# A preln graph network on one core: the mask by TensorE, more PSUM banks, ranks and single graphs at the end, and a later due time for the squares

## The chip, the cores and the metric

The kernel runs on one core of a Trainium2 chip. The metric is the device time of one execution in microseconds. A core has five engines with a queue each: TensorE (PE; its weight loads are listed as PEld), VectorE (DVE), ScalarE (ACT), GpSimd (POOL) and SyncE (SP), which here issues all DMA transfers.

## The reference

There are 128 independent graphs of 128 nodes with 256 features. Layer 0 is a gated graph network of three steps, layer 1 is graph attention, and each has a layer norm with a relu in front and a residual around it.

```python
h = relu(layernorm(x))
for i in range(3):                                   # layer 0
    m = h @ weight[i]
    aggr = einsum('bst,bsd->btd', adj != 0, m)
    h = gru_cell(aggr, h, w_ih, w_hh, b_ih, b_hh)
x = x + h
h = relu(layernorm(x))                               # layer 1
Wh = h @ W.T
e = leaky_relu((Wh @ a1)[:, :, None] + (Wh @ a2)[:, None, :], 0.2)
att = softmax(where(adj == 0, -inf, e), axis=-1)
out = x + where(adj == 0, 0, att) @ Wh
```

All data are float32; the adjacency is an int32 array of zeros and ones.

## The kernel before

**Groups.** Four graphs make a group (G = 4), so there are 32 groups (NG = 32). A group passes three recurrent steps and then an epilogue, which is layer 1. Up to six groups are alive at a time, and a fixed plan interleaves their steps. The state of a group is kept in columns: `hT` has features on the partitions and nodes along the free axis.

**The recurrent step** (`gru_step`). The products with the gate weights are done by Strassen's scheme on halves, so there are 192 blocks of seven products. Each product is a run of matmuls `128x256` (L690) into one of five fixed PSUM banks: `u`, `m7` (shown as m), `c2`, `c1_0`, `c1_1` (shown as c). ScalarE copies between banks and applies tanh (the copies at L710, L713, L721; the gates r at L743 and z at L778; the candidate at L642). VectorE adds banks (L716, L725), adds the state's half to the candidate (L785) and makes the new state `hT` in three passes (L647, L649, L651). The other three PSUM banks are a rotating room named `misc` for all other TensorE results.

**The epilogue** (`epilogue`). For the last three groups (`late`, g >= 29) all turning between layouts goes through TensorE; for the others it goes by VectorE's 32x32 transposes and a way through DRAM. The steps, with names as the profile shows them:

- `pr_o` (L489): the state turned into rows, and `xt += pr_o` (L901), the residual.
- `st_b`, `mv_b`, `norm_b` (L415, L417, L421 on VectorE, L423 to L427 on GpSimd): the statistics. `h_b` (L440): the normalised rows, on ScalarE.
- `s` (L922): the two scores of each node, products with `wa`, summed by VectorE.
- `ps` (L931): the scores of the neighbours, spread over all partitions by four TensorE transposes. For the groups before 29 this goes by way of a DRAM line.
- `e` (L958): Prelu of the sum of both scores. `A` (L967) is then turned from 0/1 into -1e30/0, and added to `e` (L969). `soft` (L975): the row maximum. `e` (L979): the exponential with its sum.
- `pp` (L988) and `prT` (L992): the attention square turned by TensorE and copied (late groups). For the others `squares_by_blocks` turns it by VectorE into `prT` and a way through DRAM: `z_e<-prT`, then `e<-z_e`.
- `pq` (L598, `gathered`): the aggregation. `hs` (L1019): its copy by ScalarE. `po` (L1027): the product with `gwt`, two graphs to a bank. `xt` or `x` (L1036): scaled and added to the residual. The rows go `out` by SyncE.

The epilogue of the last group (31) runs as two tasks of two graphs each.

**What sets the order.** An account written in the kernel (`class Order`) fixes the order of all instructions while the program is built. Every step of every task states an engine, a length, the time when its inputs are ready, and the room that it needs. The account holds a time at which each engine comes free. Tasks have ranks; at equal start the smaller rank goes first. The recurrent products are laid down one after another, and between two of them `order.fill` puts whatever can start on the other engines, and `order.matmuls` puts TensorE steps whose inputs are ready by the account:

```python
def matmuls(self, most):
    end = self.free[PE] + most
    ...
            if engine != PE or self.free[PE] >= end:
                continue
            if self.begin(PE, *needs) <= self.free[PE] + 0.05:
                self.issue(task)
```

So the account's times decide only the order. Once on the chip, each engine goes through its queue in this order and waits on semaphores. After the plan has ended, `order.finish()` lays down the rest.

For the squares the account counts four transfers of `SMALL = 0.67` us issue time, `LAND = 2.5` us, four of 0.42 and again 2.5.

Of the kernel before, what the change touches and what calls it, by code (L numbers as in the profile page):

```python
# [11 lines left out]
ALU = mybir.AluOpType  # L12
# [15 lines left out]
def preln_gnn_kernel(  # L28
# [140 lines left out]
    INF = float("inf")  # L169

    class Order:
        def __init__(self):
# [28 lines left out]
        def open(self, room, name):  # L201
            self.room_of[name] = room, self.next[room]
            self.next[room] = (self.next[room] + 1) % len(self.rooms[room])
            if room == "misc":
                return ps_misc.tile([P, T], F32, tag="misc", name=name)
            if room == "h":
                return work.tile([P, G, D], F32, tag="h", name=name, bufs=ROWS)
            if room in ("prT", "e"):
                return work.tile([P, G, P], F32, tag=room, name=name)
            if room == "x1":  # L210
                return io.tile([P, G, D], F32, tag="x1", name=name, bufs=2)
            return work.tile([P, C, T], F32, tag=room, name=name)
# [266 lines left out]

    def to_rows(hT, ready, name, pairs=range(G // 2)):  # L480

        banks = []
        t = yield PE, 0.44 * len(pairs), ready, "misc", len(pairs)
        for half in pairs:
            pt = order.open("misc", f"pr_{name}_{half}").rearrange("p (k d) -> p k d", d=D)
            for k in range(2):
                for c in range(C):
                    n = half * 2 + k
                    put(nc.tensor.transpose(  # L489
                        pt[:, k, c * P : (c + 1) * P], hT[:, c, n * P : (n + 1) * P], ident  # L490
                    ))
            banks.append(pt)
        return banks, t
# [85 lines left out]
    def rows(s, ready, name):  # L579
# [3 lines left out]
        for half, pt in enumerate(banks):  # L583
            t = yield (ACT, 0.57, ready) if half else (ACT, 0.57, ready, "h")
            order.close(f"pr_{name}_{half}", t)
            if h is None:
# [51 lines left out]
    def state(s, o, old, new, v, z, ready):  # L638
# [5 lines left out]
        if len(s.halves) == C:  # L644
# [10 lines left out]
            if s.l < NL:  # L655
# [149 lines left out]
    class Group:  # L805


        def __init__(self, g):
            self.g, self.l, self.entered, self.aT = g, 0, False, None
            (self.xt, _), (self.at, self.at_ready) = xts.pop(g), ats.pop(g)  # L810
            self.scales = scales.pop(g)
            self.kept, self.prT = [], None
            self.e = self.hs = None
            self.due = False
# [29 lines left out]
    def prologue(s):  # L844
# [27 lines left out]

    def epilogue(s, pairs, ready):

        g = s.g
        graphs = range(2 * pairs[0], 2 * pairs[-1] + 2)
# [3 lines left out]
        name = f"{g}_{pairs[0]}"  # L880
# [4 lines left out]
        end = g >= NG - 2  # L885
        e_room, hs_room = (None, None) if end else ("e", "hs")
        if late:
            banks, ready = yield from to_rows(s.hT, ready, f"{name}_o", pairs)
        else:
# [5 lines left out]
        x1 = s.x1  # L895
        for half in pairs:
            t = yield (DVE if late else DVE2), 0.62, ready
            k2 = slice(half * 2, half * 2 + 2)
            if late:
                order.close(f"pr_{name}_o_{half}", t)  # L900
                put(nc.vector.tensor_add(x1[:, k2, :], x1[:, k2, :], banks[half - pairs[0]]))  # L901
            else:
# [7 lines left out]
        one, two = v[:, 0, :], v[:, 1, :] if late else score_tiles[g % 2][:, 0:G]  # L910
        ready = t
        for i in (1, 0):
            for k in graphs:
# [6 lines left out]

                unused = s.prT[:, part.start : part.start + 2, :].rearrange("p k s -> p (k s)")
                put(nc.vector.scalar_tensor_tensor(  # L922
# [4 lines left out]
        if late:  # L927
            t = yield PE, graph_t, t, "misc"
            p2 = order.open("misc", f"ps2_{name}")
            for k in graphs:  # L930
# [73 lines left out]
        banks, ready = yield from gathered(h, prT, t, f"pq_{name}", graphs)  # L1004
        final = pairs[-1] + 1 == G // 2
        if final:
# [3 lines left out]
        for c, pq in enumerate(banks):  # L1010
            t = yield (ACT, bank_t, ready, hs_room) if s.hs is None else (ACT, bank_t, ready)
            order.close(f"pq_{name}_{c}", t)
# [8 lines left out]
        for half in pairs:  # L1021
            t = yield PE, 1.73, ready, "misc"
            po = order.open("misc", f"po_{g}_{half}").rearrange("p (k d) -> p k d", d=D)
            for j in range(2):
                k = half * 2 + j
                for c in range(C):
# [3 lines left out]
                    ))  # L1030
            if final and half == pairs[-1] and not end:
                order.close(f"hs_{g}", t)
            for j in range(2):
                k = half * 2 + j
                t2 = yield DVE, 0.4, t
                put(nc.vector.scalar_tensor_tensor(  # L1036
                    x1[:, k, :], po[:, j, :], rs[:, k : k + 1], x1[:, k, :], ALU.mult, ALU.add
                ))
            order.close(f"po_{g}_{half}", t2)
        t = yield SP, 0.45, t2  # L1040
# [93 lines left out]
    for slot, (g, l) in enumerate(plan):  # L1134
# [9 lines left out]
        last = s.state = gru_step(s, last)  # L1144
        settle(True)
    order.finish()

# [35 lines left out]
```

## Time and profile before

| | us |
|---|---|
| median of three runs | 2139.47 |
| lowest and highest run | 2136.89 and 2141.38 |
| the profiled execution | 2138.47 |
| its span in the profile | 2136.7 |
| TensorE busy in the span | 2119.0 |
| VectorE, ScalarE busy | 1724.6, 1302.4 |
| DMA, share of 16 engines' span (the queue of SyncE) | 43.9% |

The busy time of TensorE is modelled from the start of each matmul, since matmuls overlap in the array; a wait shorter than the overlap does not show as idle time. The profile has 40 slices, and the granted TensorE clock is given in each; it is at nine tenths or more in all of them, with a mean of 0.999. The kernel's lines in the views are those of the file before the change; the change shifts the later ones.

### The profile page before, as it was taken

To read this page: it belongs to the slowest core of one execution; us is meant where nothing else is said; L and a number is where in the kernel's file an instruction comes from. 1 tells how busy PE (TensorE), PEld (TensorE's weight loads), DVE (VectorE), ACT (ScalarE), POOL (GpSimd) and SP (SyncE) were. 2 spreads that over 40 slices of the span, in tenths; PEclk is the share of its full clock that TensorE was granted. 3 is DMA by queue.
4 is the path that set the end of the run, shared out by engine and by line. 5 is a ranking of instruction groups with operands and counts; after the bars stand their busy time and mean duration, and the time that the engine had idled before them with its cause. 6 is when DMAs were issued, how large, how long until landed. Compare 5 with 4: busy or idle time off the path is not lost.

```text
span 2136.7 us, 32121 instructions
## 1 busy us (share of the span) xinstructions
PE 2119.0 (99%) x10763; PEld 1879.0 (88%) x10763; DVE 1724.6 (81%) x3763; ACT 1302.4 (61%) x2855; POOL 105.9 (5%) x204
## 2 busy tenths in 40 slices
PE   9999999999999999999999999999999999999997
PEld 7888888888888888888888888888888888888886
DVE  7777888788888888888888788888878887887777
ACT  6556566566666666665666566556656665665665
POOL 2000000000000000000000000000000000000000
PEclk9999999999999999999999999999999999999999
DMA  5333454444554273544445453734445354443301
GB/s 158 64 85 81 88 118 93 110 102 92 128 110 113 59 166 68 118 94 114 101 88 129 100 123 67 156 73 115 94 109 109 85 129 102 100 94 80 83 26 40
DMA packets 667942, 211.93 MB, mean 99 GB/s; under 512 B 578304, under 2 KB 644608, under 8 KB 667776
## 3 DMA queue, kind: packets, MB, share of 16 engines
q1 hardware_dynamic: 667776, 209.87, 43.9%
q8 instruction: 85, 1.39, 0.3%
q14 instruction: 81, 0.66, 0.1%
HBM read 121.91 MB, written 87.88 MB: 98 GB/s over the span
## 4 chain that ended last, share of the span: by engine, by line
PE 96%; DMA 1%; ACT 1%; DVE 1%; SPq 1%; issue 0%; POOL 0%; DVEq 0%; ACTq 0%; POOLq 0%
PE c L690 34%; PE u L690 34%; PE m L690 11%; PE pa L598 8%; PE po L1027 5%; PE pq L598 3%; PE pw L357 1%; SPq L60 1%; DMA e<-z_e 1%; DMA z_e<-prT 0%; ACT e L979 0%; DMA wih<-in_w_ih_t 0%; ACT v L642 0%; PE pr_o L489 0%; DVE v L785 0%
## 5 line engine op out<-in xcount | busy, mean ns | idle before, releaser
L778 ACT ACTIVATE z<-c,brz 128x256 f32<-128x256 f32 x384 | 185.3, 482 | 300.1 <-PE c L690 155.4
L690 PE MATMUL u<-t_h,s_hh 128*128 128x256 f32 x1152 | 343.3, 380 | 0.5 <-DVE c L716 0.3
L690 PE MATMUL u<-t_a,s_f 128*128 128x256 f32 x1152 | 311.3, 379 | 0.0
L690 PE MATMUL c<-aT,s_f 128*128 128x256 f32 x1152 | 311.3, 379 | 0.0
L743 ACT ACTIVATE r<-c,brz 128x256 f32<-128x256 f32 x384 | 175.6, 478 | 208.4 <-PE c L690 132.0
L716 DVE TENSOR_TENSOR c<-u,m 128x512 f32<-128x512 f32 x192 | 134.0, 698 | 144.9 <-PE u L690 144.7
L690 PEld LDWEIGHTS c<-aT,s_f 128*128 128x128 f32 x1152 | 218.9, 190 | 29.8
L690 PEld LDWEIGHTS u<-t_a,s_f 128*128 128x128 f32 x1152 | 218.9, 190 | 29.8
L690 PEld LDWEIGHTS u<-t_h,s_hh 128*128 128x128 f32 x1152 | 217.3, 190 | 31.5 <-DVE c L716 1.6
L785 DVE TENSOR_TENSOR v<-v,c 128x256 f32<-128x256 f32 x384 | 154.2, 420 | 110.6 <-ACT z L778 57.7
L690 PE MATMUL c<-hT,s_hh 128*128 128x256 f32 x768 | 228.4, 379 | 0.0
L721 ACT COPY c<-u 128x512 f32<-128x512 f32 x192 | 109.4, 570 | 117.3 <-PE u L690 116.9
L713 ACT COPY m<-m 128x512 f32<-128x512 f32 x192 | 112.5, 586 | 112.0 <-PE m L690 112.0
L750 ACT ACTIVATE v<-c,bhn 128x256 f32<-128x256 f32 x384 | 172.3, 477 | 0.0
L690 PE MATMUL m<-t_h,s_hh 128*128 128x256 f32 x576 | 171.5, 379 | 0.0
L690 PE MATMUL c<-t_h,s_hh 128*128 128x256 f32 x576 | 171.3, 379 | 0.0
L690 PEld LDWEIGHTS c<-hT,s_hh 128*128 128x128 f32 x768 | 145.8, 190 | 19.8
L725 DVE TENSOR_TENSOR c<-u,m 128x512 f32<-128x512 f32 x192 | 132.0, 687 | 37.5 <-ACT c L721 36.0
L690 PE MATMUL m<-t_a,s_f 128*128 128x256 f32 x576 | 155.6, 379 | 0.0
L690 PE MATMUL u<-aT,s_f 128*128 128x256 f32 x576 | 155.6, 379 | 0.0
L690 PE MATMUL c<-t_a,s_f 128*128 128x256 f32 x576 | 155.6, 379 | 0.0
L710 ACT COPY c<-u 128x512 f32<-128x512 f32 x192 | 109.5, 570 | 53.3 <-PE u L690 53.3
(125 smaller groups left out, 3900.0 us busy)
## 6 DMA issues: line engine op xcount, KB each, us to landing
z<-tq SPq DMA_DIRECT2D x248, 128.0 KB
h<-z SPq DMA_DIRECT2D x248, 128.0 KB
xt<-in_x SPq DMA_DIRECT2D x31, 512.0 KB
z_a<-tq_a SPq DMA_DIRECT2D x120, 128.0 KB
hT_a<-z_a SPq DMA_DIRECT2D x120, 128.0 KB
z_b<-tq_b SPq DMA_DIRECT2D x116, 128.0 KB
h_b<-z_b SPq DMA_DIRECT2D x116, 128.0 KB
x<-in_x SPq DMA_DIRECT2D x29, 512.0 KB
```

The lines of the kernel that those rows point to most:

```text
L598: put(nc.tensor.matmul(pa[:, k * P : (k + 1) * P], h[:, k, c * P : (c + 1) * P], A[:, k, :], start=True, stop=True,))
L690: put(nc.tensor.matmul(to(q), S[0][:, gate_no, weight, :], moving, start=first and q == 0 and i == 0, stop=(i == len(ends) - 1), skip_grou ...
L710: put(nc.scalar.copy(c1[0], u))
L713: put(nc.scalar.copy(m, m7))
L716: put(nc.vector.tensor_tensor(c2, u, m, ALU.add))
L721: put(nc.scalar.copy(c1[1], u))
L725: put(nc.vector.tensor_tensor(c22, u, m, ALU.add))
L743: put(nc.scalar.activation(r[:, o, cols], src, AF.Tanh, bias=brz[:, o : o + 1], scale=0.5))
L750: put(nc.scalar.activation(v[:, o, cols], src, AF.Identity, bias=bhn[:, o : o + 1], scale=0.5))
L778: put(nc.scalar.activation(z[:, o, cols], src, AF.Tanh, bias=brz[:, C + o : C + o + 1], scale=0.5))
L785: put(nc.vector.tensor_tensor(v[:, o, cols], v[:, o, cols], src, ALU.add))
L1027: put(nc.tensor.matmul(po[:, j, :], hs[:, c, k * P : (k + 1) * P], gwt[:, c, :], start=(c == 0), stop=(c == C - 1),))
```

## The change

The diff has six parts.

1. **The mask by TensorE** (groups 30 and 31, `end`). The mask is turned into -1e30/0 by a task of its own (`mask`, rank 1) that the account places from 5 us before the state is done. A matmul of the identity with the mask opens the bank of the scores, and the neighbours' scores are then ordinary matmuls that accumulate onto it. The add of the mask to `e` on VectorE is gone for these two groups. The transposes of the scores become ordinary matmuls in group 29 too.
2. **More banks at the end.** Once the last recurrent step is laid down, its five banks join the room `misc`, which then has eight.
3. **Ranks.** The epilogues of groups 30 and 31 have rank 1.8 and that of group 29 has 1.9, in place of 2.
4. **Single graphs in group 31**: `po`, its output add and its store go graph by graph, and the second `hs` of each half is copied by VectorE. The halves of the group stay: graphs 0 and 1, and graphs 2 and 3; pairs are now named by lists of graphs.
5. **Squares.** In `squares_by_blocks` the account's time for the landing of the turned square is 2.0 us later. This concerns groups 0 to 28.
6. `to_rows` counts its length by graphs, which gives the same numbers for pairs.

```diff
+    more = u, m7, c2, *c1
...
+            if room == "misc" and self.room_of[name][1] > 2:
+
+                return more[self.room_of[name][1] - 3].rearrange("p n t -> p (n t)")
...
 (squares_by_blocks)
-        return (yield from by_way_of_dram(
+        t = yield from by_way_of_dram(
             tmp.rearrange("p q k a -> p (q k) a"), lambda: e.rearrange("p k s -> p (k s)"),
             G, t, f"{name}_e",
-        ))
+        )
+        return t + 2.0
...
-                pairs = range(G // 2)
-                for p in [pairs] if s.g < NG - 1 else [pairs[:1], pairs[1:]]:
-                    order.add(2, epilogue(s, p, max(s.halves)))
+                if s.g >= NG - 2:
+                    s.off_ready = INF
+                    order.add(1, mask(s, max(s.halves) - 5.0))
+
+                for graphs in [range(G)] if s.g < NG - 1 else [range(2), range(2, 4)]:
+                    order.add((1.8 if s.g >= NG - 2 else 1.9 if s.g == NG - 3 else 2), epilogue(s, graphs, max(s.halves)))
...
+    def mask(s, ready):
+
+        t = s.off_ready = yield DVE, 0.36, ready
+        put(nc.vector.tensor_scalar(s.A, s.A, -1.0, BIG, ALU.add, ALU.mult))
+        return t
...
-            t = yield PE, graph_t, t, "misc"
+            t = yield PE, 4 * graph_t if end else graph_t, max(t, s.off_ready), "misc"
             p2 = order.open("misc", f"ps2_{name}")
+            if end:
+
+                put(nc.tensor.matmul(
+                    p2[:, cols], ident, s.A[:, part, :].rearrange("p k s -> p (k s)"),
+                    start=True, stop=False, skip_group_check=True,
+                ))
             for k in graphs:
-                put(nc.tensor.transpose(
-                    p2[:, k * P : (k + 1) * P], two[:, k : k + 1].to_broadcast([P, P]), ident
+                put(nc.tensor.matmul(
+                    p2[:, k * P : (k + 1) * P], two[:, k : k + 1].to_broadcast([P, P]), ident,
+                    start=not end, stop=True, skip_group_check=True,
                 ))
...
-        off_ready = yield DVE, 0.36 * n / G, ready
-        off = s.A[:, part, :]
-        put(nc.vector.tensor_scalar(off, off, -1.0, BIG, ALU.add, ALU.mult))
-        t = yield DVE2, row_t, max(t, off_ready) - HOP
-        put(nc.vector.tensor_tensor(le, le, off, ALU.add))
+        if not end:
+            off_ready = yield from mask(s, ready)
+            t = yield DVE2, row_t, max(t, off_ready) - HOP
+            put(nc.vector.tensor_tensor(le, le, s.A, ALU.add))
...
+            on = DVE if c and final_one else ACT
+            t = yield (on, bank_t, ready, hs_room) if s.hs is None else (on, bank_t, ready)
...
-            put(nc.scalar.copy(hs[:, c, cols], pq[:, cols]))
+            copy = nc.vector.tensor_copy if on == DVE else nc.scalar.copy
+            put(copy(hs[:, c, cols], pq[:, cols]))
...
-        for half in pairs:
-            t = yield PE, 1.73, ready, "misc"
-            po = order.open("misc", f"po_{g}_{half}").rearrange("p (k d) -> p k d", d=D)
+        for ks in twos(graphs) if not final_one else [range(k, k + 1) for k in graphs]:
+            t = yield PE, 0.865 * len(ks), ready, "misc"
+            po = order.open("misc", f"po_{g}_{ks[0]}").rearrange("p (k d) -> p k d", d=D)
...
+            if final_one:
+                yield SP, 0.45, t2
+                dma(out[g * G + k], x1[:, k, :])
+        if final_one:
+            return
...
+    order.rooms["misc"] += [max(order.free[PE], t) for t in (banks["u"], *3 * [0.0], banks["c1_1"])]
     order.finish()
```

More of the change, by code (lines that the diff above doesn't have):

```diff
@@ L478, in to_columns, with twos, to_rows @@
         return hT, t
-    def to_rows(hT, ready, name, pairs=range(G // 2)):
+    def twos(graphs):
+        return [graphs[i : i + 2] for i in range(0, len(graphs), 2)]
+    def to_rows(hT, ready, name, graphs=range(G)):
         banks = []
-        t = yield PE, 0.44 * len(pairs), ready, "misc", len(pairs)
-        for half in pairs:
-            pt = order.open("misc", f"pr_{name}_{half}").rearrange("p (k d) -> p k d", d=D)
-            for k in range(2):
+        t = yield PE, 0.22 * len(graphs), ready, "misc", len(twos(graphs))
+        for two in twos(graphs):
+            pt = order.open("misc", f"pr_{name}_{two[0]}").rearrange("p (k d) -> p k d", d=D)
+            for k, n in enumerate(two):
                 for c in range(C):
-                    n = half * 2 + k
                     put(nc.tensor.transpose(
@@ L584, in rows @@
             t = yield (ACT, 0.57, ready) if half else (ACT, 0.57, ready, "h")
-            order.close(f"pr_{name}_{half}", t)
+            order.close(f"pr_{name}_{2 * half}", t)
             if h is None:
@@ L811, in __init__ @@
             self.scales = scales.pop(g)
+            self.off_ready = 0.0
             self.kept, self.prT = [], None
@@ L871, in place_of_e, with epilogue @@
         ).rearrange("p (k s) -> p k s", s=P)
-    def epilogue(s, pairs, ready):
+    def epilogue(s, graphs, ready):
         g = s.g
-        graphs = range(2 * pairs[0], 2 * pairs[-1] + 2)
         n = len(graphs)
@@ L879, in epilogue @@
         cols = slice(part.start * P, part.stop * P)
-        name = f"{g}_{pairs[0]}"
+        name = f"{g}_{graphs[0]}"
         bank_t, row_t, graph_t = 0.57 * n / G + 0.02, 0.62 * n / G + 0.02, 0.11 * n
         late, h = g >= NG - 3, None
-        end = g >= NG - 2
+        end, final_one = g >= NG - 2, g == NG - 1
         e_room, hs_room = (None, None) if end else ("e", "hs")
         if late:
-            banks, ready = yield from to_rows(s.hT, ready, f"{name}_o", pairs)
+            banks, ready = yield from to_rows(s.hT, ready, f"{name}_o", graphs)
         else:
@@ L895, in epilogue @@
         x1 = s.x1
-        for half in pairs:
-            t = yield (DVE if late else DVE2), 0.62, ready
-            k2 = slice(half * 2, half * 2 + 2)
+        for i, two in enumerate(twos(graphs)):
+            t = yield (DVE if late else DVE2), 0.31 * len(two), ready
+            k2 = slice(two[0], two[-1] + 1)
             if late:
-                order.close(f"pr_{name}_o_{half}", t)
-                put(nc.vector.tensor_add(x1[:, k2, :], x1[:, k2, :], banks[half - pairs[0]]))
+                order.close(f"pr_{name}_o_{two[0]}", t)
+                put(nc.vector.tensor_add(
+                    x1[:, k2, :], x1[:, k2, :], banks[i][:, 0 : len(two), :]
+                ))
             else:
@@ L911, in epilogue @@
         ready = t
+        place = min(part.start, G - 2)
         for i in (1, 0):
@@ L919, in epilogue @@
                     s.prT = order.open("prT", f"prT_{g}")
-                unused = s.prT[:, part.start : part.start + 2, :].rearrange("p k s -> p (k s)")
+                unused = s.prT[:, place : place + 2, :].rearrange("p k s -> p (k s)")
                 put(nc.vector.scalar_tensor_tensor(
@@ L927, in epilogue @@
         if late:
-            t = yield PE, graph_t, t, "misc"
+            t = yield PE, 4 * graph_t if end else graph_t, max(t, s.off_ready), "misc"
             p2 = order.open("misc", f"ps2_{name}")
+            if end:
+                put(nc.tensor.matmul(
+                    p2[:, cols], ident, s.A[:, part, :].rearrange("p k s -> p (k s)"),
+                    start=True, stop=False, skip_group_check=True,
+                ))
             for k in graphs:
-                put(nc.tensor.transpose(
-                    p2[:, k * P : (k + 1) * P], two[:, k : k + 1].to_broadcast([P, P]), ident
+                put(nc.tensor.matmul(
+                    p2[:, k * P : (k + 1) * P], two[:, k : k + 1].to_broadcast([P, P]), ident,
+                    start=not end, stop=True, skip_group_check=True,
                 ))
@@ L1004, in epilogue @@
         banks, ready = yield from gathered(h, prT, t, f"pq_{name}", graphs)
-        final = pairs[-1] + 1 == G // 2
+        final = graphs[-1] + 1 == G
         if final:
@@ L1010, in epilogue @@
         for c, pq in enumerate(banks):
-            t = yield (ACT, bank_t, ready, hs_room) if s.hs is None else (ACT, bank_t, ready)
+            on = DVE if c and final_one else ACT
+            t = yield (on, bank_t, ready, hs_room) if s.hs is None else (on, bank_t, ready)
             order.close(f"pq_{name}_{c}", t)
@@ L1018, in epilogue @@
             hs = s.hs
-            put(nc.scalar.copy(hs[:, c, cols], pq[:, cols]))
+            copy = nc.vector.tensor_copy if on == DVE else nc.scalar.copy
+            put(copy(hs[:, c, cols], pq[:, cols]))
         ready = t
-        for half in pairs:
-            t = yield PE, 1.73, ready, "misc"
-            po = order.open("misc", f"po_{g}_{half}").rearrange("p (k d) -> p k d", d=D)
-            for j in range(2):
-                k = half * 2 + j
+        for ks in twos(graphs) if not final_one else [range(k, k + 1) for k in graphs]:
+            t = yield PE, 0.865 * len(ks), ready, "misc"
+            po = order.open("misc", f"po_{g}_{ks[0]}").rearrange("p (k d) -> p k d", d=D)
+            for j, k in enumerate(ks):
                 for c in range(C):
@@ L1030, in epilogue @@
                     ))
-            if final and half == pairs[-1] and not end:
+            if final and ks[-1] == graphs[-1] and not end:
                 order.close(f"hs_{g}", t)
-            for j in range(2):
-                k = half * 2 + j
+            for j, k in enumerate(ks):
                 t2 = yield DVE, 0.4, t
@@ L1038, in epilogue @@
                 ))
-            order.close(f"po_{g}_{half}", t2)
+            order.close(f"po_{g}_{ks[0]}", t2)
+            if final_one:
[3 more added lines that the diff above has]
+            return
         t = yield SP, 0.45, t2
```

## The prediction

> **What bounds the kernel now.** The times are those of one profiled execution: 2138.47 us on the device, 2136.7 us of it span, so 1.8 us lie around the span. The median of the runs shown, 2139.47, is 1.0 us above it. All sums below start from 2138.47; "faster" and "slower" are against 2139.47, and 0.2% of that, 4.3 us, is about what a measurement of this kernel can tell from no change.
>
> The first view to read is the head of the page.
>
> ```profile
> span 2136.7 us, 32121 instructions
> PE 2119.0 (99%) x10763; PEld 1879.0 (88%) x10763; DVE 1724.6 (81%) x3763; ACT 1302.4 (61%) x2855; POOL 105.9 (5%) x204
> ```
>
> TensorE is busy for all but 17.7 us. So an edit can gain only where TensorE waits, and every instruction added to it costs its own length unless it falls into such a wait. The second view is the busy time by stretches of the span; its columns are PE, PEld, DVE, ACT, POOL, the granted clock (PEclk), DMA.
>
> ```profile
> 0.00:20.00 20.00, 17.24 (x65) 11.70 (x66) 11.41 (x43) 9.56 (x23) 3.19 (x12) 1.00 0.89 276
> ...
> 100.00:2000.00 1900.00, 1896.82 (x9670) 1691.80 (x9669) 1547.34 (x3311) 1167.34 (x2545) 84.54 (x162) 1.00 0.46 102
> ...
> 2101.00:2137.00 36.00, 24.56 (x126) 18.93 (x124) 23.78 (x77) 16.88 (x52) 2.66 (x6) 0.95 0.13 45
> ```
>
> The waits are 2.8 us at the start (not touched), 3.2 us in the 1900 us of the middle, and 11.4 us after the last recurrent product. The third view says who ends them: columns are total us, number, longest.
>
> ```profile
> ...
> PEld pq L598 <- DMA e<-z_e: 5.1, 5, 2.2
> ...
> PE pp L988 <- ACT e L979: 4.3, 3, 2.7
> PE pq L598 <- DMA e<-z_e: 3.0, 4, 1.8
> PE pq L598 <- ACT prT L992: 2.3, 4, 0.7
> ```
>
> In the middle it is one thing: the matmul pq waits for the turned square e to come back from DRAM. The other two rows belong to the end. The chain that ended last shows the end in order (start, length, what):
>
> ```profile
> 2083.08 1.78 PE pq L598 x16
> ...
> 2098.70 2.60 PE c L690 x12
> ...
> 2106.13 3.60 PE pq L598 x16
> 2109.73 0.45 PE pr_o L489 x4
> ...
> 2120.58 3.29 PE po L1027 x14
> ...
> 2132.60 0.48 DVE xt L1036
> ```
>
> The last recurrent product ends at 2101.30. The last row is the first of two output adds; the second ends at 2133.47 in the timeline, 32.2 us after 2101.30. These 32.2 us are the tail. The same sixteen pq instructions take 1.78 us at 2083 and 3.60 at 2106. Short stretches say why:
>
> ```profile
> 2102.60:2106.00 3.40, 1.31 (x4) 0.55 (x4) 3.26 (x6) 2.98 (x11) 0.00 (x0) 1.00 0.00 0
> 2106.00:2109.40 3.40, 3.27 (x15) 3.27 (x16) 3.17 (x12) 0.67 (x2) 0.00 (x0) 0.50 0.00 0
> ...
> 2112.80:2116.20 3.40, 2.21 (x11) 1.47 (x9) 3.37 (x8) 2.03 (x7) 1.25 (x3) 1.00 0.00 0
> ```
>
> After 3.4 us with TensorE busy for 1.31, the clock is granted at 0.50 for the next 3.4. After 3.4 us with 2.21 busy it is not. The half-speed stretch cost 3.60 - 1.78 = 1.8 us, and it delayed the transposes pr_o that everything of group 31 waits for.
>
> **1. Squares 2.0 us later in the account.** The account (not the chip) decides behind which recurrent product pq is queued. One product is six records in 1.29 us. Two more microseconds put pq one or two products later, 1.3 to 2.6 us. The price of the waits: the PE row shows 3.0 us in four. A 128x256 record is 0.38 long while records start 0.216 apart (1.29 / 6), so each gap is shown 0.16 too short: 3.0 + 4 x 0.16 = 3.6, and the fifth wait, which only the PEld row counts, is about 0.3 more. That makes 4.0 us; the ends are 3.0 (PE row) and 5.1 (PEld row). The longest wait, 1.8 + 0.16, could leave 0.7 behind if pq moves by one product only. I take -4.0. The edit renumbers the whole schedule from group 2 on, transfers included: in SyncE's queue the loads of x and of the adjacency change places with the line of scores. The recurrent TensorE work of the middle is the same, instruction for instruction. New waits are taken at nothing, because in the profile no other load is waited for by TensorE in the middle; their bound is one wait such as the longest, +2.
>
> **2. What TensorE gets more of.** A transpose of 128x128 is one record of 0.11 us (pr_o, four in 0.45). An ordinary f32 matmul is two (pq, eight matmuls, sixteen records in 1.78). The score transposes of groups 29, 30 and 31 become ordinary matmuls: 4 x 0.11 = 0.44 more each. The mask matmul of 512 columns is not in the trace; twice a 256-column matmul (2 x 2 x 0.216) is 0.87, for groups 30 and 31. Together 3 x 0.44 + 2 x 0.87 = 3.1 us. In the changed program's order, pp and pq of group 29 (0.44 + 1.78) stand in front of the last recurrent product, where they stood behind it, and so do group 29's scores. That product therefore ends 2.22 + 0.44 = 2.66 us later. The rest of the additions fall into the tail.
>
> **3. The tail by steps**, from the end of the last recurrent product, durations from the rows of the same instructions before. One half of the last tanh (0.6) now runs ahead of the last z, so the three passes that make hT end at 5.45 instead of 6.02. The transposes pr_o find TensorE idle (it has done po of group 29 at 1.73, into a bank of its own): 0.60 + 0.04, to 6.1; before, they waited for pq until 8.43. Add and statistics of two graphs on VectorE take 2.18 (2110.20 to 2112.38), to 8.3; those of the other two, now queued directly behind, to 10.4. Group 30's maximum 0.68, four exponentials 1.7, last transpose and copy 1.0: 13.8. Here the mask's add (0.68) is gone and its tensor_scalar (0.42) is done earlier, in VectorE's wait for the transposes. Then TensorE works without pause: pq30 1.78, half of po29 1.73, half of po30 1.73, pp31 0.22, mask and scores of the last pair 0.87: 20.1. Two Prelu 0.63, maximum 0.42, two exponentials 0.89 and hand-offs 0.2: 22.3; TensorE meanwhile has 2.6 us of po30 and pq31, to 22.7. Then pp 0.22, one graph of po 0.87, pq 0.89, three graphs of po 2.6, drain 0.15: 27.4. The last add begins there and ends 0.5 later: 27.9, against 32.2 before. The same adding-up comes out 0.6 short for the tail of before, so I make it 28.5. The two halves of hs on VectorE instead of ScalarE, and four stores of one graph instead of two of two, are taken at nothing; the last store is smaller, the issues 0.4 each are hidden between adds 0.87 apart; bounds -0.5 and +0.5.
>
> TensorE's clock comes on top. The new order leaves TensorE idle for 3.7 us before pr_o and for about 3 before pp of group 30, longer than the 2.7 that halved the clock before. One half-speed stretch does 1.7 us of work in 3.4: +1.7 at most, of which 0.7 hides behind VectorE if it falls on group 30's scores. None costs 0, two cost 3.4; I take 1.4. Tail: 28.5 + 1.4 = 29.9, 2.3 less than 32.2.
>
> A page speaks against this order: the Trainium skill, "TensorE: Matmul & The Clock Gate", Part 1 (the HAM clock gate) says that a window of about 3.4 us without matmuls halves the clock and that a busy window restores it, the windows running freely. The trace agrees on the length, 3.4 us at 0.50; it is stricter in that 1.31 us of modelled work in the window did not prevent it. By the page alone only a wholly empty window would count, and the sum would be 1.4 lower.
>
> **Sum.** 2138.47 - 4.0 + 2.66 - 2.3 = 2134.8. The end itself is about even (2.66 - 2.3 = +0.4); the gain is the squares.
>
> **The rivals.** *The clock decides the end.* Idle stretches of 3.7 and 3 us each close the gate, the second on the unbroken run pq30 to scores of group 31: 2 us more than taken, 2136.8. For it: both gaps exceed the earlier one. Against it: the phase of the stretches is a matter of chance, and the stretch with 2.21 us of work stayed at full clock. *The waits stay.* If pq moves by one product only and the transfers it waits for move along with it, only the end counts: 2138.9. Against it: the waits before are mostly far below one product. *The end runs at full clock*, and the runs away from the profiled one lose more than 4.0 to the squares (their median is 1.0 higher): 2133. *Slower: another load becomes the late one.* The state in columns, hT_a, comes back through DRAM in the same SyncE queue. In the new order its first reader on VectorE (L458 before) stands closer behind its load in every third group. VectorE is strictly in order and 81% busy, so the wait holds back the sums c (L716) that TensorE's next product needs. Seven groups of about 1.5 us would be 10 us: 2145. It decides as soon as that load lands after its reader's turn by more than about a microsecond; for it speaks only that SyncE's queue changes everywhere, against it that no such wait stands in the profile and TensorE itself needs that state tens of microseconds later.
>
> **How the numbers follow.** Forecast (squares' waits gone, end about even) 0.62: of it 0.48 lie below 2135.2 and 0.14 above. Full clock at the end 0.07, faster. Clock decides 0.17 and waits stay 0.05, both within 0.2%. Another load late 0.09, slower. So faster 0.55, within 0.36, slower 0.09. The range: -4.0 may be -5.1 and the clock 0 instead of 1.4, with 0.8 for the stores and the run's own spread: 2131.5. Upwards the clock's 2 us, the wait that stays 0.7 and a new wait of 2: 2139.5. The slow rival and thin ends, under 2 in 10, stay outside.
>
> **What would show it.** Right: no row of pq waiting for e<-z_e, PE idle below 1 us between 100 and 2000; the last recurrent product ends 1 to 2 us earlier than 2101.3 (2.66 later by work, 4.0 earlier by waits); last add 29 to 31 us after it; PEclk 0.50 in a stretch of the last 30 us. Wrong: DVE or PE waiting for hT_a or h loads in the middle, pq still waiting, or a second half-speed stretch under pq of group 30.

## The result and the profile after

| | before | after |
|---|---|---|
| median (22 runs each, taken in turn), us | 2138.63 | 2142.02 |
| lowest and highest run | 2136.89 and 2142.62 | 2139.37 and 2146.18 |
| span of the profiled execution | 2136.7 | 2139.7 |
| last recurrent product ends | 2101.30 | 2106.64 |
| from there to the end of the last add (the tail) | 32.2 | 30.3 |

The changed kernel takes 1.0014 times as long (95% interval 1.0008 to 1.002): 3.4 us slower. The forecast was 2134.8, with a range up to 2139.5. The last two rows say where it went: the tail is shorter, as forecast (29.9), but it begins 5.3 us later, where the forecast had it begin 1.3 us earlier.

The head of the page after:

```profile
span 2139.7 us, 32130 instructions
PE 2119.6 (99%) x10781; PEld 1881.5 (88%) x10781; DVE 1724.7 (81%) x3761; ACT 1301.5 (61%) x2853; POOL 104.2 (5%) x204
```

TensorE has 18 records more and 3.0 us more span, yet only 0.6 us more busy time. The busy time by stretches (PE first; the clock, the DMA share and GB/s at the end of a row):

```profile
100.00:2000.00 1900.00, 1893.50 (x9648) 1687.66 (x9648) 1545.21 (x3307) 1165.67 (x2545) 84.31 (x162) 1.00 0.46 102
2101.00:2140.00 39.00, 28.42 (x150) 24.22 (x148) 25.33 (x77) 16.76 (x47) 2.27 (x6) 0.91 0.16 54
```

The middle was to lose less than 1 us; it loses 6.5, against 3.2 before. (The middle is the stretch from 100 to 2000 us.) Who ends the waits (total us, number, longest; lines after the change are 5 to 27 higher, so pq is L607, the sums c L727, the first sums of a step's state t_h L463):

```profile
PEld pq L607 <- DMA e<-z_e: 5.9, 5, 1.5
...
DVE t_h L463 <- DMA hT_a<-z_a: 5.6, 5, 2.2
...
PE pq L607 <- DMA e<-z_e: 4.0, 5, 1.1
...
PE u L497 <- DVE hT L660: 3.7, 1, 3.7
...
PE u L701 <- DVE c L727: 2.7, 3, 1.5
```

Three things stand here. pq still waits for e, as long as before. A wait is new that stood in no view before: VectorE at t_h for hT_a, five times, and TensorE's recurrent products then wait for VectorE's sum c. The 3.7 us ahead of pr_o is in the tail and was foreseen. Counted from the start of one matmul to the start of the next, beyond the usual 0.216 us, the middle loses 3.98 us at pq before; after, it loses 4.83 at pq and 3.63 where products wait for c (0.19 of the latter stood before too).

The end, by the chain of work that ended last (start, length, what):

```profile
2105.33 1.31 PE c L701 x6
...
2112.09 0.67 PE u L497 x4
...
2118.18 1.63 PE c L1013 x4
...
2121.52 3.02 PE pq L607 x16
...
2136.45 0.48 DVE xt L1062
```

pr_o (L497) starts 5.45 us after the last product and ends at 6.12, the times of the forecast. pq of group 30 takes 3.02 us instead of 1.78; short stretches show the clock:

```profile
2108.40:2111.80 3.40, 0.00 (x0) 0.00 (x0) 3.33 (x3) 0.00 (x0) 0.00 (x0) 1.00 0.00 0
2111.80:2115.20 3.40, 2.85 (x18) 2.18 (x18) 3.12 (x11) 0.23 (x1) 0.11 (x1) 1.00 0.00 0
2115.20:2118.60 3.40, 0.42 (x2) 0.21 (x2) 3.09 (x11) 2.96 (x11) 2.16 (x6) 0.79 0.00 0
2118.60:2122.00 3.40, 3.40 (x14) 2.82 (x14) 2.18 (x10) 2.21 (x8) 0.00 (x0) 0.50 0.05 18
2122.00:2125.40 3.40, 3.40 (x19) 3.30 (x19) 2.06 (x9) 2.57 (x8) 0.00 (x0) 0.71 0.41 141
```

The 3.7 us ahead of pr_o left the clock at 1.00. The 3.25 us ahead of pp were followed by half speed: the clocks of the last three rows (0.79, 0.50, 0.71) add up to 6.8 us of it.

**Why the squares' waits stayed.** The transfers of SyncE around one square, before (group 8). VectorE has turned the square into prT at 768.63 + 0.70 = 769.33:

```profile
769.21 1.71 SPq L60 DMA_DIRECT2D h<-z  x4
770.97 2.57 SPq L60 DMA_DIRECT2D z_e<-prT  x4
```

Here z_e is issued 1.6 us after the square is ready, behind one step of h. After (group 10), the square is turned at 895.61 + 0.70 = 896.31:

```profile
880.18 4.80 SPq L60 DMA_DIRECT2D z_b<-tq_b  x4
887.80 1.26 SPq L60 DMA_DIRECT2D h_b<-z_b  x3
889.17 2.98 SPq L60 DMA_DIRECT2D z_a<-tq_a  x4
892.19 3.55 SPq L60 DMA_DIRECT2D z<-tq  x4
895.91 2.49 SPq L60 DMA_DIRECT2D hT_a<-z_a  x4
...
899.55 3.02 SPq L60 DMA_DIRECT2D h<-z  x4
902.67 2.60 SPq L60 DMA_DIRECT2D z_e<-prT  x4
```

Here z_e is issued 6.4 us after the square is ready, behind hT_a, out, h_b and h: a burst, transfers that SyncE issues one directly behind another. The same burst makes hT_a late: its columns were turned at 886.26 (the tq_a before it in VectorE's queue), but SyncE stood at h_b until z_b had landed, issued z_a 2.9 us late, and then z before hT_a. VectorE and TensorE, in the timeline (idle time before, and what ended it, in brackets):

```profile
902.75 0.76 DVE L463 TENSOR_TENSOR t_h<-hT_a 128x256 f32<-128x256 f32 x2 [2.22 <-DMA hT_a<-z_a]
```

```profile
908.56 0.70 PE L701 MATMUL u<-t_h,s_hh 128*128 128x256 f32 x2 [1.52 <-DVE c L727]
```

### The profile page after: what moved, and what is told of

Its sections match the earlier page's. It is cut to its first block, busy times and chain, and to the rows that moved or that the text cites. A ratio compares the mean times of both kernels' runs of the same rounds, so it can differ in the third digit from the quotient of the medians.

```text
span 2139.7 us, 32130 instructions
## 1 busy us (share of the span) xinstructions
PE 2119.6 (99%) x10781; PEld 1881.5 (88%) x10781; DVE 1724.7 (81%) x3761; ACT 1301.5 (61%) x2853; POOL 104.2 (5%) x204
## 2 busy tenths in 40 slices
DMA packets 667973, 211.92 MB, mean 99 GB/s; under 512 B 578336, under 2 KB 644640, under 8 KB 667808
## 5 line engine op out<-in xcount | busy, mean ns | idle before, releaser
L727 DVE TENSOR_TENSOR c<-u,m 128x512 f32<-128x512 f32 x192 | 134.0, 698 | 141.7 <-PE u L701 132.7
```

Source lines behind the costliest of these rows:

```text
L727: put(nc.vector.tensor_tensor(c2, u, m, ALU.add))
```

## The experiments

The theory tested (R, regrouping): the 2.0 us do not leave the transfers in place, they regroup SyncE's queue, so that in one group in three z_e and hT_a stand behind a longer burst. The first rival: the parts at the end cost the time. The second: the waits follow the room, the extra time that the account grants the square. For the end, theory C says that the half-speed clock is on the path.

| kernel | median | ratio to before (95%) | last product | tail |
|---|---|---|---|---|
| `sq1_alone` | 2134.73 | 0.9976 (0.9967 to 0.9985) | 2098.3 | 32.2 |
| `sq15_alone` | 2156.94 | 1.0079 (1.0064 to 1.0094) | 2114.3 | 32.3 |
| `sq2_alone` | 2145.32 | 1.0023 (1.0013 to 1.0033) | 2106.0 | 32.6 |
| `end_alone` | 2143.66 | 1.0016 (1.0008 to 1.0025) | 2098.9 | 39.5 |
| `sq1_then_2` | 2135.05 | 0.9977 (0.9969 to 0.9986) | 2099.3 | 31.2 |
| `z_pool` | 2138.57 | 0.9998 (0.9989 to 1.0006) | 2104.0 | 31.5 |
| `zb_pool` | 2137.02 | 0.9989 (0.998 to 0.9998) | 2102.9 | 30.4 |
| `za_pool` | 2146.74 | 1.0033 (1.0024 to 1.0043) | 2108.3 | 31.5 |
| `warm` | 2132.73 | 0.9968 (0.9956 to 0.9979) | 2101.3 | 28.2 |
| `mask_add` | 2133.43 | 0.9973 (0.9962 to 0.9985) | 2099.6 | 30.4 |
| `pairs_end` | 2135.89 | 0.9984 (0.9975 to 0.9992) | 2099.5 | 31.1 |
| `warm_add` | 2132.37 | 0.9965 (0.9952 to 0.9977) | 2097.9 | 27.8 |
| `held5` | 2131.47 | 0.9958 (0.9944 to 0.9972) | 2093.9 | 33.6 |
| `held5_warm` | 2132.12 | 0.9962 (0.9949 to 0.9974) | 2091.9 | 35.7 |

The last two columns are of one profiled execution each; the place of the last product varies by some 2 us with the loads at the start (2099.3 in `sq1_then_2`, 2101.3 in `warm`, with no wait in the middle of either). The kernels were timed on several chips, each beside the kernel before, so the ratios are what can be compared.

### The squares alone: 1.0, 1.5 and 2.0 us

```diff
 (before, squares_by_blocks)
-        return (yield from by_way_of_dram(
+        t = yield from by_way_of_dram(
...
-        ))
+        )
+        return t + 1.0
```

`sq15_alone` and `sq2_alone` have 1.5 and 2.0 in that place.

> The kernel before with part 5 alone (squares 2.0 us later in the account). Theory R, regrouping: the 2.0 us do not leave the transfers where they were; they regroup SyncE's queue so that z_e is issued 5 to 6 us after the square is turned (1.4 to 2.8 before). It expects about five waits of pq for e, 4 to 5 us together, in other groups than before, and VectorE's waits for hT_a that reach TensorE, 3 to 4 us; the last recurrent product about 3 us later than before, at 2104, and the tail near 32, so about 2142, 0.1 to 0.2% slower. The rival, the end costs it: the squares help or do nothing, and the time lies between 2134.5 and 2138.6.

> The kernel before with squares 1.0 us later in the account instead of 2.0. In the program's order pq moves by one recurrent product (1.3 us) while SyncE's queue keeps the order of before. Theory R expects the waits of pq for e to go, or to keep at most 0.7 us together, no wait for hT_a, the last recurrent product 3 to 4 us earlier, at 2097.5 to 2098.5, and the tail of before: about 2135, 0.15 to 0.2% faster. The rival, the waits follow whatever room the account grants: 3 to 4 us of waits of pq stay and the time is that of before within 1.5 us.

> The kernel before with squares 1.5 us later in the account, between the 1.0 that gave 2134.7 and the 2.0 that gave 2145.3. Theory R: what counts is the place of z_e in SyncE's queue, not the room granted. At 1.5 the program's order has z_e behind the same burst of transfers as at 2.0, in every third group (8, 11, 14 and so on), and pq stands one recurrent product nearer to it; so the eight waits of pq for e are longer than at 2.0, 1 to 2.3 us each: 2144 to 2154. The rival, room: the time lies between those of 1.0 and 2.0 or below, 2134 to 2143.

`sq2_alone` has the changed kernel's middle, without its end, and is 0.23% slower than before:

```profile
PE pq L599 <- DMA e<-z_e: 4.9, 5, 1.6
...
DVE t_h L458 <- DMA hT_a<-z_a: 4.2, 5, 2.1
```

From start to start pq loses 5.7 us there. Not all of the 0.23% is the middle: pp and pq of group 29 (20 records, 2.22 us by the forecast's prices) stand ahead of the last product in `sq2_alone` too, and its tail is no shorter for it. `sq1_alone` is 0.24% faster than before, and SyncE's 1490 transfers stand in its trace in the order of before, one for one. Between them, 1.5 is the slowest of all. The waits for e, of 1.0 and of 1.5:

```profile
PE pq L599 <- DMA e<-z_e: 0.4, 1, 0.4
```

```profile
PE pq L599 <- DMA e<-z_e: 11.9, 7, 2.4
```

The median of 1.5 is 2.9 us above what was expected at most, and its profiled run was the quickest of five, so the row understates it. The landings, in the one group of three that is late (from group 5 to group 23), counted from the moment when VectorE has turned the square:

| squares | z_e issued | e landed | pq's turn |
|---|---|---|---|
| 0 (before) | 1.4 to 2.8 | 10 to 11 | 10.3 |
| 1.0 | 1.4 to 3.1 | 9.8 to 11.2 | 11.6 |
| 1.5 | 4.8 to 6.4 | 13.4 to 15.2 | 11.9 |
| 2.0 | 5.4 to 6.5 | 14.0 to 14.7 | 13.2 |

pq's turn is its start less TensorE's waits in that group. Group 2, the first of the pattern, is not in the table: there z_e is issued 4.0 us after the square is turned and e lands at 12.2 before; with 1.0 it is 3.4 and 12.0. It had the longest wait before (1.8) and has the one that is left at 1.0 (0.4). For the other groups one product more (1.3 us) was all that the waits needed. At 1.5 the queue has the other order and e comes 3 to 4 us later, while pq moves hardly further; at 2.0 pq gets its second product, and the waits are shorter again. So the room granted is not what counts, and the second rival has fallen.

### The end alone, and both with 1.0

```diff
 (after, squares_by_blocks)
-        return t + 2.0
+        return t + 0.0
```

```diff
 (after, squares_by_blocks)
-        return t + 2.0
+        return t + (1.0 if int(name) < 25 else 2.0)
```

> The changed kernel with the squares' 2.0 us set to 0: parts 1 to 4 and 6 alone. The middle is that of before: waits of pq for e of 3 to 4 us, none for hT_a. Theory R, with the order of this program: pq and po of group 28, which keeps rank 2, come last of all behind group 31, and the last recurrent product has about 2.6 us less in front of it than in the changed kernel; so it ends at 2101 to 2102 or earlier, and the tail is 36 us or more: 2140 to 2144. The rival, the end parts are about even as the prediction had it: 2137.5 to 2139.5.

> The changed kernel with squares 1.0 us later up to group 24 and 2.0 us from group 25: SyncE's queue then keeps the order of before in the middle, and the end has the order of the changed kernel. Theory R expects no waits of pq for e above 0.7 us together and none for hT_a, the last recurrent product 7 to 8 us earlier than in the changed kernel (its 4.8 us of waits for e and 3.6 for hT_a gone), at 2098 to 2099.5, and the same tail of 30.3 us: 2133 to 2135. The rival, the waits belong to the end's new order or follow the room: the time stays within 2 us of the changed kernel's 2142.

`sq1_then_2` is the changed kernel but for SyncE's order in the middle, which is again that of before, and for pq, which stands one product earlier. It has no wait of pq for e and none for hT_a, and it is 0.23% faster than before. TensorE's busy time in the middle:

```profile
100.00:2000.00 1900.00, 1899.96 (x9689) 1696.09 (x9688) 1551.56 (x3316) 1169.48 (x2556) 84.37 (x162) 1.00 0.46 102
```

That is the forecast's kernel, at the forecast's time. Beside it on the same chip, `sq1_alone`, which has none of the end's parts, is as fast (2134.73 against 2135.05): the end is even within the intervals, as forecast. Only the tail was 0.9 longer than expected; its two half-speed stretches come to 10.2 us, against 6.8 in the changed kernel, and `warm` below shows what they cost.

`end_alone` shows what the end's parts do without the squares' shift. There pq and po of group 28, which keeps rank 2, slide behind group 31, and the tail is 39.5 us.

### Which queue: transfers moved from SyncE to GpSimd

```diff
 (after, by_way_of_dram)
+        on = nc.gpsimd if n == G else nc.sync
...
-            dma(z[:, :, i, :], tmp[i * 32 : (i + 1) * 32])
+            put(on.dma_start(z[:, :, i, :], tmp[i * 32 : (i + 1) * 32]))
...
-            dma(to_[q * 32 : (q + 1) * 32], rows_[q])
+            put(on.dma_start(to_[q * 32 : (q + 1) * 32], rows_[q]))
```

`za_pool` has `n == G or name.startswith("a")`, which adds z_a and hT_a; `zb_pool` has `"b"`, which adds z_b and h_b instead. The queues of TensorE, VectorE and ScalarE are those of the changed kernel.

> The changed kernel (squares 2.0), where the eight transfers of each square, z_e and e, are issued by GpSimd instead of SyncE; the account still counts them as SyncE's, so the order of TensorE, VectorE and ScalarE is unchanged. Theory R, z_e stands too late in SyncE's queue: pq's waits for e in groups 7, 10, 13 and so on go, those for hT_a shrink, since eight issues fewer stand in that queue, and the last recurrent product ends 4 to 8 us earlier than 2106.6: 2134 to 2138. The rival, transfers in flight or DRAM are the limit: the square lands as late as before, and the time stays at 2142. A third way: GpSimd's issues are slow or hold up its part of the statistics, which shows as waits for norm; then the time rises and nothing is told about SyncE.

With z_e and e on GpSimd, no wait for e is left on TensorE. The waits for hT_a did not shrink as expected, since nothing was taken from ahead of them:

```profile
DVE t_h L463 <- DMA hT_a<-z_a: 6.1, 5, 2.0
```

The time, 0.16% below the changed kernel's ratio, is 0.6 us above what was expected.

> The changed kernel (squares 2.0), where GpSimd issues z_e and e, and z_a and hT_a too; the order of TensorE, VectorE and ScalarE is unchanged. With the squares alone on GpSimd the waits of pq for e were gone and VectorE's for hT_a stood (6.1 us), which cost TensorE some 3 us. Theory R expects those for hT_a to go too, PE idle below 1 us between 100 and 2000, the last recurrent product at 2099 to 2101.5 and 2134 to 2136.5. The rival, hT_a is late for a reason other than SyncE's queue (its data, DRAM): its waits stay and the time is 2137.5 to 2139.5. GpSimd's issues could hold up its statistics; that would show as waits for norm.

This one missed: the waits for hT_a grew to 11.2 us. GpSimd itself waited 54.5 us for z_a to land, and z_a took 4.4 us from issue to landing there (median). What was named as a sign of GpSimd's issues holding up its statistics came too: ScalarE's h_b waited 32.8 us for GpSimd's norm_b, against 7.3 in the changed kernel. So the run told nothing about SyncE.

> The changed kernel (squares 2.0), where GpSimd issues z_e and e, and z_b and h_b; z_a and hT_a stay on SyncE, and the order of TensorE, VectorE and ScalarE is unchanged. In the changed kernel SyncE stands at h_b until z_b has landed, and z_a is issued 2.9 us after its data is ready (889.17 against 886.26). Theory R: without z_b and h_b ahead, z_a and hT_a are issued some 3 us earlier, VectorE's waits for hT_a (6.1 us with the squares alone on GpSimd) fall below 1.5 us, PE idle between 100 and 2000 falls from 3.6 to below 1.5 us: 2134.5 to 2137. The rival, hT_a is late for a reason other than SyncE's queue: its waits stay at 5 to 7 us, 2138 to 2140. If h_b comes late by way of GpSimd, waits of the residual add for it show, and the time rises.

SyncE's queue around the same group as above:

```profile
886.00 2.92 SPq L517 DMA_DIRECT2D z_a<-tq_a  x4
888.96 4.43 SPq L517 DMA_DIRECT2D z<-tq  x4
893.56 2.41 SPq L526 DMA_DIRECT2D hT_a<-z_a  x4
```

z_a is issued 3.2 us earlier than in the changed kernel (889.17) and hT_a 2.4 us earlier (the rows just ahead of them stand 0.3 us earlier as well). No wait of VectorE for hT_a is left at all, and none of pq for e. One other wait came in the middle: at 1865 us ScalarE's Prelu stands 2.7 us for the line of scores, and TensorE behind it 2.0. So the time is at the upper edge of what was expected, and its ratio is 0.25% below the changed kernel's, some 5 us. Both halves of the middle's loss come from the places in SyncE's queue. One thing is not separated by these runs: GpSimd's transfers carry the same bytes in fewer packets (493,510 in all against 667,973), which may help the square. hT_a stayed on SyncE in its own packets, and the rows show its earlier issue.

### The end: clock, mask, single graphs, held work

`warm` adds matmuls whose result nobody reads. They run in one of the recurrent step's banks:

```diff
 (sq1_then_2)
+    def warm(n, ready):
+        for _ in range(n):
+            yield PE, 0.43, ready
+            put(nc.tensor.matmul(
+                c1[1].rearrange("p n t -> p (n t)")[:, 0:D], ident, gwt[:, 0, :], start=True, stop=True,
+            ))
...
+    for n, ready in ((6, order.free[PE]), (6, order.free[PE] + 8.0)):
+        order.add(3, warm(n, ready))
     order.finish()
```

> The kernel squares 1.0 then 2.0, with twelve extra TensorE matmuls of 128x256 whose result nobody reads: six behind the last product of group 29 and six ahead of pp of group 30, where TensorE stands idle for 3.7 and 2.6 us. Every other engine's queue is unchanged. Theory C, the half-speed clock of the end is on the path: no stretch below 0.9 in the last 40 us, sixteen pq of group 30 back from 3.4 to 1.8 us, and a tail of 27.5 to 29 us in place of 31.2, so 2131.5 to 2133. The rival, the half-speed stretches lie beside VectorE's statistics and adds: the clock is full, but the time falls by less than 1 us, 2134 to 2135.

The clock is full to the end, pq of group 30 takes 1.85 us, and the tail is 28.2 in place of 31.2. The stretch with that pq, in `sq1_then_2` and in `warm`:

```profile
2114.60:2118.00 3.40, 3.40 (x19) 3.40 (x18) 2.06 (x9) 2.19 (x6) 0.00 (x0) 0.54 0.46 159
```

```profile
2114.60:2118.00 3.40, 3.40 (x27) 3.27 (x26) 2.73 (x12) 3.40 (x10) 0.00 (x0) 1.00 0.41 145
```

The runs show less of it (ratio 0.9968 against 0.9977, intervals that overlap). The programs with the changed kernel's end order bear it out: with 6.8 us at half speed the tails are 30.3 and 30.4 (the changed kernel, `zb_pool`), with 10.2 us they are 31.2 to 31.5 (`sq1_then_2`, `z_pool`, `za_pool`). Against the 28.2 of `warm`, the clock costs that end 2.1 to 3.3 us.

```diff
 (sq1_then_2, epilogue: mask_add)
-            t = yield PE, 4 * graph_t if end else graph_t, max(t, s.off_ready), "misc"
+            t = yield PE, graph_t, t, "misc"
...
-        if not end:
-            off_ready = yield from mask(s, ready)
-            t = yield DVE2, row_t, max(t, off_ready) - HOP
-            put(nc.vector.tensor_tensor(le, le, s.A, ALU.add))
+        off_ready = s.off_ready if end else (yield from mask(s, ready))
+        t = yield DVE2, row_t, max(t, off_ready) - HOP
+        put(nc.vector.tensor_tensor(le, le, s.A[:, part, :], ALU.add))
```

The matmul of the mask is gone and the scores are transposes again.

> The kernel squares 1.0 then 2.0, with the mask of groups 30 and 31 added by VectorE again (0.68 us, and 0.42 for each half of 31) and their neighbours' scores by transposes; the mask's turning into -1e30/0 stays early. TensorE has 3.0 us less work, and half of po of group 29 now stands ahead of pp of group 30. Theory E, TensorE's work behind pp of group 30 sets the end and VectorE's add only delays its start: 1 to 2.5 us faster, 2132.5 to 2134. The rival, the mask by TensorE pays as meant, since VectorE's adds stand in the chain of group 30 and of 31: 0.7 to 1.5 us slower, 2135.8 to 2136.6.

```diff
 (sq1_then_2, epilogue: pairs_end)
-            on = DVE if c and final_one else ACT
+            on = ACT
...
-        for ks in twos(graphs) if not final_one else [range(k, k + 1) for k in graphs]:
+        for ks in twos(graphs):
...
-            if final_one:
-                yield SP, 0.45, t2
-                dma(out[g * G + k], x1[:, k, :])
-        if final_one:
-            return
```

> The kernel squares 1.0 then 2.0, with po, add and store of group 31 by pairs again and both copies of hs on ScalarE (part 4 undone). The order of all engines ahead of the last pp is the same. Single graphs let the last add begin half a po (0.87 us) earlier and make the last store smaller: expected 0.4 to 1.2 us slower than with single graphs, 2135.4 to 2136.3. The rival, the copy on VectorE and the four stores cost as much as they give: within 0.3 us.

The mask by VectorE does not show as slower: the tail is 30.4 against 31.2, and the time lies where theory E had it. With pairs in place of single graphs the tail is the same (31.1) and the time lies where it was expected. But the intervals of `warm`, `mask_add` and `pairs_end` all overlap that of `sq1_then_2`, so the sizes are not settled, and the rival that the mask by TensorE pays is not excluded.

`warm_add` is `mask_add` with the twelve matmuls of `warm`.

> The kernel squares 1.0 then 2.0 with both of the edits that gained: the mask added by VectorE, and twelve idle matmuls that keep the clock. If the two gains (1.6 and 2.3 us) are separate, 2130.5 to 2131.5. If both only shortened the same stretch, the half-speed run of TensorE behind pp of group 30, 2131.8 to 2133.

The median lies in the range of the second case. At full clock the tail is 27.8 with the add and 28.2 with the mask by TensorE: of the 0.8 us between the tails of `sq1_then_2` and `mask_add`, 0.4 are left. The other 0.4 did not come from less time at half speed, which is 10.2 us in both; what they came from stays open.

`held5` is `mask_add` with no other TensorE work between the last five products (`HELD` is 5):

```diff
 (mask_add, product)
-            order.matmuls(1.0)
+            s.products += 1
+            if (s.g, l) != plan[-1] or s.products <= 14 * l + 14 - HELD:
+                order.matmuls(1.0)
```

> The kernel squares 1.0 then 2.0 with the mask added by VectorE, and with no other TensorE work between the last five recurrent products: pp, pq and po of groups 28 and 29 stand behind them, where TensorE waited for the state of group 31 and for group 30's exponentials. The last product should end 5 to 7.5 us earlier, at 2092 to 2094, the idle stretches be filled with real work, and the clock stay full. Theory C and E together: 2128.5 to 2131. The rival, the work moved behind the last product lengthens the tail by all of its length: 2132 to 2134.

The last product ends at 2093.9 as expected, but the tail is 33.6: of the 5.7 us moved behind the product, 3.2 came back in the tail. The median is 0.5 above what was expected and below the rival. It is the lowest of all, 0.42% below the kernel before, though not told apart from `warm` and `warm_add`. The clock did not stay full: behind an idle stretch of 2.2 us it was granted at 0.56 from 2105.6 to 2109.0.

`held5_warm` adds four such matmuls, into bank u, ahead of the scores of group 30.

> The kernel held5 with four extra TensorE matmuls of 128x256, whose result nobody reads, in its one idle stretch of 2.2 us ahead of the scores of group 30; in held5 that stretch was followed by a stretch at 0.56 of the clock, in which eight po took 3.07 us instead of 1.73. Theory C: the clock stays full and the end comes 0.5 to 1.5 us earlier, 2130 to 2131. The rival, VectorE sets that part of the end: no change, 2131 to 2132.

No gain. The first stretch is now at full clock, but a later one is not:

```profile
2109.00:2112.40 3.40, 1.76 (x6) 0.75 (x6) 3.08 (x16) 3.13 (x13) 0.00 (x0) 0.86 0.00 0
2112.40:2115.80 3.40, 3.32 (x15) 3.33 (x16) 3.23 (x12) 1.65 (x7) 0.00 (x0) 0.50 0.04 16
```

The half-speed run was moved, not removed, and it is longer: 6.8 us against 3.4 in `held5`. Whether VectorE sets this end anyway is not settled by it.

## Why the prediction was wrong

**1. The squares, -4.0: this step failed.** Its first half held: pq's turn moved by two products (2.6 us) and a little more, from 10.3 to 13.2. What failed is "New waits are taken at nothing", with a bound of +2. In place of a gain of 4.0 the middle lost 0.9 more at pq and 3.6 at the sums c: 4.5. The step kept the landing of e in place while it moved pq, although it named that the edit renumbers the transfers of SyncE too. The profile of before showed no late hT_a because its order had none. What it did show is that in one group in three e landed close to pq's turn (from 0.3 us before it to 0.7 behind, and 1.9 behind in group 2). The order of the queue behind which it lands stands in the changed program in full; z_e's and hT_a's places in that order had to be read against the issue lengths (1.7 to 4.8 us for four in the rows above).

**The slower rival** named this mechanism, hT_a read by VectorE behind its load in every third group, and what waits for it. Its price of seven waits of 1.5 was too high (five waits, 5.6 us on VectorE, 3.6 on TensorE); its chance stood at 0.09. **"The waits stay"** had the other half, transfers that move along with pq; it stood at 0.05 since the waits were "mostly far below one product". They did go with one product and the transfers in place, as `sq1_alone` shows but for 0.4 us; at 1.5 and 2.0 the transfers stood in another order.

**2. TensorE's work ahead of the last product, +2.66.** The trace has the 24 records that the step names ahead of the product: four of pp, sixteen of pq, four of the scores. The twenty of pp and pq stand ahead of it in `sq2_alone` and in `end_alone` too, so each half of the change is enough to bring them there. Busy time up to the product's end, which is modelled, rose from 2094.70 to 2096.84 us: +2.1. The remaining 3.2 of the 5.3 us are idle time. The mask matmul of 512 columns, costed at 0.87 from two halves, takes 0.86 from its start to the next in `warm`.

**3. The tail, 28.5 at full clock and 1.4 for the clock.** `warm` has 28.2, and its pq of group 30 starts 13.8 us after the last product, the time of the step. The clock's 1.4 was too small: 2.1 to 3.3, by the comparison above. The rival that the clock decides had half of its mechanism: in the changed kernel the second gap was followed by half speed on that run and the first was not, and the tail lies 30.3 - 28.2 = 2.1 above that of `warm`.

**The end about even, +0.4:** held within the noise, +0.3 between the medians of `sq1_alone` and `sq1_then_2`, whose intervals overlap.

**The clock.** The Trainium skill, "TensorE: Matmul & The Clock Gate", Part 1, has free-running windows and a clock that halves after an idle one. That they run freely agrees with the rows above: 3.7 us of idle time passed without harm and 3.25 us did not. That a window must be idle does not: the 3.41 us just ahead of the fall to half speed held 1.31 us of modelled work before (from 2102.57 on), 1.18 in the changed kernel (from 2113.75) and 1.86 in `held5_warm` (from 2108.03). Cut into such windows, forward and back from a fall, the ends of the profiled executions show how much is enough: every window with up to 1.41 us of modelled work was followed by half speed and every one with 1.89 or more by full speed, while between 1.43 and 1.86 both occur. The 3.7 us gap lay on two windows, which held 1.43 us (from 2106.92) and 1.66 us (from 2110.34) of work.

**Not tried:** another rank for group 28, and the banks of part 2 alone.

## What to carry to other kernels

When an account orders several queues at once, a due time is no local dial: read the place of each dependent transfer in the DMA queue of the changed program, and compare its issue and landing with the reader's turn, for each group of the pattern. Try the smallest shift that moves the reader by one step, and check that the transfer queue's order is still the same. An idle stretch of TensorE near the end can cost twice, once as a wait and once as half speed behind it (6.8 us at half speed behind 3.25 us here). Matmuls that nobody reads kept the clock full in `warm` and took 3.0 us off the tail; in `held5` and `held5_warm` a half-speed stretch stayed, so look at the clock of every stretch after such an edit.

## What the runs showed of the hardware

Four transfers of one step take SyncE 1.7 to 4.8 us to issue (h 1.71, z_a 2.98, z 3.55 and z_b 4.80 in the rows above), and in a queue with such bursts in it each of them delays everything behind. What makes one longer than another is not shown. The Trainium skill, "DMA: Bandwidth & Descriptors", section "Issuing engines are not separate DMA queues", says that issuing from several engines only saves the issuing sequencer's time, which is usually small against the transfer. Here that time was not small: four issues of z_e took 2.60 us, and one such transfer took 2.4 us from issue to landing in `z_pool` (median). Taking two round trips (z_e and e, z_b and h_b) off SyncE brought 0.25%, some 5 us, with the same bytes moved. But GpSimd is no free place for them: with z_a and hT_a there it waited 54.5 us for landings, held up ScalarE's h_b for 32.8 us, and the kernel was 0.35% slower than with the square alone there.
